# A new head for an attention and density kernel: 4 KB load rows, own tiles for the first keys, nine maxima moved into the stream, summed weights for the offsets

## The chip, the cores and the metric

The kernel runs on one core of a Trainium2 chip. The metric is device time in microseconds (us) of one execution. Engines are named as in the profile: PE (matrix products), PEld (its weight loads, which overlap PE), DVE (vector), ACT (scalar), POOL (GpSimd), SP (issues DMAs). ACT and POOL issue DMAs as well. Each engine runs its own instructions in program order and waits on semaphores for others.

## The reference

The input is `x`, 8 images of 192 channels and 64 x 64 = 4096 pixels, float32. Two layers, each added to its input; only the first is touched by the change.

```python
def _L0_conv_ref(x, w1, b1, a1, w2, b2, a2, wa, ba, aa):
    q = prelu(conv1x1(x, w1, b1), a1)      # 24 channels
    k = prelu(conv1x1(x, w2, b2), a2)      # 24 channels
    v = prelu(conv1x1(x, wa, ba), aa)      # 192 channels
    q = q.reshape(b, -1, hw).transpose(0, 2, 1)
    k = k.reshape(b, -1, hw)
    score = softmax(einsum('bnc,bcm->bnm', q, k), axis=2)
    v = v.reshape(b, c, hw).transpose(0, 2, 1)
    out = einsum('bnm,bmc->bnc', score, v)
    return out.transpose(0, 2, 1).reshape(b, c, h, w)

x = x + _L0_conv_ref(_gn(x), ...)
x = x + _L1_conv_ref(_gn(x), ...)
```

`_gn` normalises each of 32 groups of six channels by its mean and variance over all pixels. `_L1_conv_ref` pushes each value, once lowered and once raised by 0.5, through a chain of small per-channel layers with tanh and takes the absolute difference of two sigmoids.

## The kernel before

**Layout.** The 192 channels are held as 64 rows of three (`g`), and the pixels as two halves (`s`), so that 2 x 64 partitions are used. An image is cut into eight column parts `d` of 256 pixels per half; two parts make a chunk `c` of 512. A program planned step by step in Python (`at`, `job`, `work_off`) decides the order in which instructions stand on each engine; nothing is reordered on the chip.

**Head.** For the first image all is made at once. SP loads the eight parts (L97, two DMAs of 64 rows x 3 x 256 columns each) into buffers of the later density stage. `norm_stat` (L516) takes statistics, `norm_end` turns them into mean and scale `nrm` through two tiny products. `weights` (L603) scales the weights `wr` and `wa_sb` by `nrm` on ACT (L612), and computes the offsets that the mean gives to keys, queries (`bk`) and values (`ba`) by products over the three groups (L622, L627), with the already scaled weights. `keys` (L661) makes queries and keys of one part: products (L669), two Relus on ACT (L679), a DVE step (L684), and a split into a rounded part `kh` (L690, ACT) and its rest `kq` (L695, POOL); both go to DRAM (`kqd`, L687, on SP's queue). `fetch_keys` (L738) and `queries` (L722) read them back into four ring tiles `kr` and a tile `q`, in the layout of the score products. `values` (L771) makes a part's values: 24 products (L786), the offset added on DVE out of the product bank (L795), the slope on DVE (L800).

**Maxima.** Before a block of 512 queries can be scored, each query's largest score is needed. A block takes 16 maxima, each two products into a bank pair `mx` (L825) and one reduce on DVE (L833). `max_end` (L853) turns 16 of them into `rn`, stores it to DRAM (`nd`, L867) and reads it back as two rows of `q` (L871). The first maxima are made in the head, two at a time in the tiles `sc_head` and `mx_head`: `LEAD` = 25 of them.

**Stream.** 1024 steps `t`, 128 for an image, 16 for a block. In step `t` PE makes the scores of step `t + 1` (L896), one maximum of step `t + LEAD` (L825), and the attention of step `t` (L912, sixteen passes of 193 columns); ACT makes the exponentials (L901); DVE the reduce. Around them stand, by due times and credits, the loads, statistics, weights, keys and values of the next image, and on DVE, ACT and POOL the density layer of the image before. The credits take a job's PE time as room for DVE and ACT work (2.0 for the offset products). The `mx` tile exists once, and so does `sc`. The main loop is at L1634; small parameters of the density layer (`parameters`, L242) are computed in image 0 from step 4 on, from 22 table loads that SP issues in the head (L222).

**Completion of DMAs.** SP's and ACT's DMAs share eight completion semaphores; a DMA that gets one whose last user is under way is issued when that one has landed. An issue waits in its queue, and so does all behind it.

Of the kernel before, what the change touches and what calls it, by code (L numbers as in the profile page):

```python
# [18 lines left out]
def kernel(  # L19
# [30 lines left out]
    nc = tc.nc  # L50
# [70 lines left out]


    for d in range(NP):
        xi["first", 0, d] = bufs[3 + d][:, 0 : 3 * P].rearrange("p (g n) -> p g n", g=3)
        load(xi["first", 0, d], 0, d, P)

# [22 lines left out]
    wa_sb = const.tile([128, 3, C], F32, name="wa_sb")  # L149
    ba_all = const.tile([128, C], F32, name="ba_all")  # L150
    vslope = const.tile([128, 1], F32, name="vslope")
    nslope = const.tile([128, 1], F32, name="nslope")
# [7 lines left out]
    sa = st[:, 6 * CR : 6 * CR + 3 * C].rearrange("p (g o) -> p g o", g=3)  # L160
    sb = st[:, 6 * CR + 3 * C : 6 * CR + 4 * C]
    for s in range(2):
        p = slice(R * s, R * s + R)
        nc.scalar.dma_start(out=s1[p], in_=w1t.rearrange("(r g) o -> r g o", g=3))
        nc.scalar.dma_start(out=s2[p], in_=w2t.rearrange("(r g) o -> r g o", g=3))
        nc.scalar.dma_start(out=sa[p], in_=wat.rearrange("(r g) o -> r g o", g=3))
    nc.scalar.dma_start(out=sb, in_=ba.partition_broadcast(128))
    for k in range(4):
        b_ = b1 if k // 2 else b2
        nc.scalar.dma_start(out=bb[32 * k : 32 * k + CR], in_=b_.unsqueeze(1))  # L170
    for k in range(2):
        a = a1 if k else a2
        nc.scalar.dma_start(out=slope[64 * k : 64 * k + 64], in_=a.partition_broadcast(64))
    nc.scalar.dma_start(out=vslope, in_=aa.partition_broadcast(128))

# [12 lines left out]
    def spread():  # L188

        for k in range(4):  # L190
            p = slice(R * (k % 2), R * (k % 2) + R)
            nc.gpsimd.tensor_copy(wr[p, :, 32 * k : 32 * k + CR], (s1 if k // 2 else s2)[p])
        for g in range(3):
            nc.gpsimd.tensor_scalar(
                wa_sb[:, g, :].rearrange("p (h r) -> p h r", h=3),
                sa[:, g, :].rearrange("p (r h) -> p h r", h=3), vsign, None, ALU.mult,
            )
        nc.gpsimd.tensor_scalar(
            ba_all.rearrange("p (h r) -> p h r", h=3),
            sb.rearrange("p (r h) -> p h r", h=3), vsign, None, ALU.mult,  # L200
        )
# [12 lines left out]

    mm, cb, ff = table(24), table(10), table(9)
    for src, dst, at, n in (
        (m0, mm, 0, 3), (m1, mm, 3, 9), (m2, mm, 12, 9), (m3, mm, 21, 3),
# [385 lines left out]
    def weights(b, then):  # L603
# [3 lines left out]
        def scale():  # L607
            for k, src in (("k", wr), ("v", wa_sb)):
# [3 lines left out]
                nc.scalar.activation(d, src, AF.Copy, scale=res[:, 1:2])  # L612
            mb = cell["mb"] = fold.tile([128, 128], F32, tag="mb", name=f"mb_{b}")

            nc.vector.tensor_scalar(
                mb, res[:, 0:1].to_broadcast([128, 128]), 0.5, None, ALU.mult
            )

        def products():
            pf = cell["pf"]  # L620
            for g in range(3):
                cell["write"](nc.tensor.matmul(  # L622
                    pf[:, 0:2], lhsT=wf["k", b][:, g, :], rhs=res[:, 0:2],
                    start=g == 0, stop=g == 2,
                ))
            for g in range(3):
                cell["write"](nc.tensor.matmul(  # L627
                    pf[:, 4 : 4 + C], lhsT=cell["mb"], rhs=wf["v", b][:, g, :],
                    start=g == 0, stop=g == 2,
                ))  # L630

# [28 lines left out]

    def keys(b, d, what, done):  # L661

# [3 lines left out]
        def make(pk):  # L666
# [6 lines left out]
            done()  # L673
            kq = work.tile([128, P], F32, tag="kq", bufs=3, name=f"kq_{b}_{d}")
            kh = work.tile([128, P], F32, tag="kh", bufs=2, name=f"kh_{b}_{d}")

# [33 lines left out]

        job(make, d % 2)

# [57 lines left out]

    def values(b, d, what, done):  # L771

# [4 lines left out]
        def make(pv):  # L777
# [19 lines left out]
            def last():  # L797
# [3 lines left out]
                made.update(("v", b, d, k) for k in range(2))  # L801

            return [
                (0, lambda: None, 0.0, 0.0, 2.3), (1, first, 1.0, 0.0, 0.0),
                (2, last, 1.0, 0.0, 0.0),
            ]

        job(make, 0 if at_once else 1, 1 if what == "v" else 3, 2)

# [772 lines left out]

    for d in range(NP):
        for k in range(2):
# [12 lines left out]

    norm_end((0, 0), 2 * NP, 0, lambda: weights(0, lambda: None))
    settle()

    todo = [(keys, 2 * c + h) for c in ORDER for h in range(2)]
    todo += [(values, 2 * c + h) for c in ORDER for h in range(2)]
    ahead = deque([] for _ in range(13))
    ahead.extend(list(range(m, min(m + 2, LEAD))) for m in range(0, LEAD, 2))
    while todo or ahead:
        if todo:
            make, d = todo.pop(0)
            make(0, d, "first", lambda: None)
        if any(list(ahead)[:3]):
            del homes[2:]  # L1610
        pair = list(zip(others, ahead.popleft() if ahead else ()))
        for t, m in pair:
            max_products(*place(m), t)
        for t, m in pair:
            max_reduce(*place(m), t)
        if STEPS - 1 in [m for _, m in pair]:
            max_end(0, 0)
# [4 lines left out]
        if (0, 0) in kept and (0, 0) not in qt:  # L1622
            queries(0, 0)
        go_on()
    settle()
    assert not due and not loads
    now[0] = 0
    rest = parameters()
    stream[0] = True

    RATE = 4.15
    moves = plan_keys()
    scores(0)()
    for t in range(last):  # L1634
# [23 lines left out]
        attend(t)  # L1658
        work_off(t, RATE - 1.215)
    t = last  # L1660
# [42 lines left out]
```

## Time and profile before

| | |
|---|---|
| runs | 4350.76, 4351.48, 4351.46 us; median 4351.46 |
| profiled execution | 4350.1 us, span from the first to the last instruction 4348.1 |
| granted TensorE clock, mean | 0.986 of full speed |
| busy, share of the span | PE 97%, PEld 88%, DVE 89%, ACT 66%, POOL 26% |
| last load of the first image used by statistics | 20.67 us |
| first key product / first maximum / first score product | 30.0 / 63.4 / 104.5 us |

A view of stretches gives the busy time of each engine in it; the chain of work goes back from the last instruction, at each step to what released it; the timeline lists instructions in order of time, with the idle time before each and what ended it in brackets.

### The profile page before, as it was taken

The page shows a single profiled execution, that of the slowest core. Times are in us where ns is not written, and L with a number is a line of the kernel's source. Part 1 is how long each engine was busy: PE and PEld are TensorE (multiplying, and loading weights), DVE is VectorE, ACT ScalarE, POOL GpSimd, SP SyncE. Part 2 cuts the span into 40 slices and gives each one's busy share as a digit, 9 for nine tenths or more (in the row PEclk, how much of TensorE's full clock was granted, in tenths as well). Part 3 has the DMA queues.
Part 4 walks back from the last instruction along what each step waited for, and adds up shares of the span by engine and source line. Part 5 has one row for each costly group of instructions (what it writes and reads, how often), then busy time and mean ns, then how long its engine had stood idle before and what let it go on. Part 6 is the DMA issues. An engine that isn't in the chain of part 4 may idle for free.

```text
span 4348.1 us, 59628 instructions
## 1 busy us (share of the span) xinstructions
PE 4217.4 (97%) x23464; PEld 3810.4 (88%) x23464; DVE 3883.2 (89%) x4055; ACT 2848.1 (66%) x3104; POOL 1118.2 (26%) x1204
## 2 busy tenths in 40 slices
PE   7999999999999999999999999999999999999796
PEld 4999999999999999999999999999999998999432
DVE  5444359999999998999999999999999999999999
ACT  1333337776777767677677767777677767778775
POOL 1000001432223322342233322243133323333100
PEclk7999999999999999999999999999999999999898
DMA  3201133245343444336333442435333442324100
GB/s 80 43 26 42 37 73 71 67 83 98 76 83 75 93 97 83 64 65 118 80 87 67 86 108 62 88 76 105 83 82 71 87 92 52 70 48 73 25 15 15
DMA packets 239113, 309.55 MB, mean 71 GB/s; under 512 B 91249, under 2 KB 164849, under 8 KB 238833
## 3 DMA queue, kind: packets, MB, share of 16 engines
q1 hardware_dynamic: 201472, 173.15, 17.9%
q0 software_dynamic: 36288, 132.14, 17.3%
q8 instruction: 184, 3.01, 0.3%
q14 instruction: 97, 0.79, 0.1%
q10 hardware_dynamic: 1072, 0.47, 0.1%
HBM read 131.34 MB, written 42.21 MB: 40 GB/s over the span
## 4 chain that ended last, share of the span: by engine, by line
PE 55%; DVE 35%; ACT 4%; issue 3%; DMA 2%; POOL 1%; SPq 0%; DVEq 0%; POOLq 0%; ACTq 0%
PE b L912 37%; DVE d L1186 20%; DVE rm L833 9%; PE sc L896 7%; PE mx L825 7%; PE b L786 2%; DVE st L516 2%; PE b L669 1%; ACT e L901 1%; DMA xi<-in_x_dram 1%; DVE d L1144 1%; DVE xc L957 1%; DVE v L800 1%; DVE v L795 1%; DMA nd<-rn 0%
## 5 line engine op out<-in xcount | busy, mean ns | idle before, releaser
L912 PE MATMUL b<-v,e 128*128 128x193 f32 x16384 | 2844.8, 327 | 0.0
L912 PEld LDWEIGHTS b<-v,e 128*128 128x128 f32 x16384 | 2729.6, 190 | 90.7
L901 ACT ACTIVATE e<-sc 128x1024 f32<-128x1024 f32 x1024 | 1044.8, 1020 | 1198.4 <-PE sc L896 1194.2
L833 DVE TENSOR_REDUCE rm<-mx 128x1 f32<-128x1024 f32 x999 | 1216.2, 1217 | 369.9 <-PE mx L825 369.2
L1186 DVE SCALAR_TENSOR_TENSOR d<-d,un,d 128x1024 f32<-128x1024 f32 x1008 | 1302.2, 1312 | 14.7 <-ACT d L1180 8.8
L1186 DVE SCALAR_TENSOR_TENSOR d<-d,rt,d 128x1024 f32<-128x1024 f32 x684 | 875.7, 1293 | 6.6 <-PE b L1125 0.8
L896 PE MATMUL sc<-q,kr 98*128 98x512 f32 x2048 | 781.1, 462 | 12.3 <-ACT e L901 9.5
L1180 ACT ACTIVATE d<-d,bn,wn 128x1024 f32<-128x1024 f32 x504 | 617.7, 1235 | 69.5 <-DVE d L1186 68.8
L825 PE MATMUL mx<-kr,q 96*128 96x512 f32 x1998 | 637.3, 400 | 18.4 <-DVE rm L833 17.1
L1172 POOL DMA_DIRECT2D d<-xc x252 | 220.1, 906 | 1231.1 <-ACT d L1167 977.9
L825 PEld LDWEIGHTS mx<-kr,q 96*128 96x128 f32 x1998 | 370.2, 189 | 134.4 <-DVE rm L833 50.7
L1377 POOL MEMSET pause<- 128x1 f32 x456 | 61.6, 135 | 1313.6 <-DVE d L1186 1313.5
L896 PEld LDWEIGHTS sc<-q,kr 98*128 98x128 f32 x2048 | 355.1, 191 | 39.0 <-ACT e L901 20.2
L1158 ACT ACTIVATE d<-xc,bn,wn 128x1024 f32<-128x1024 f32 x288 | 349.9, 1232 | 7.6 <-DVE bn L582 7.6
L1228 POOL TENSOR_TENSOR d<-d,d 128x512 f32<-128x512 f32 x168 | 325.7, 1940 | 39.5 <-ACT d L1222 38.2
L1167 ACT ACTIVATE d<-d,un 128x1024 f32<-128x1024 f32 x252 | 282.2, 1141 | 0.0
L695 POOL TENSOR_TENSOR kq<-kq,kh 128x256 f32<-128x256 f32 x64 | 85.3, 1333 | 380.3 <-ACT kh L690 379.7
L1429 POOL TENSOR_TENSOR d<-d,d 128x512 f32<-128x512 f32 x80 | 161.0, 2012 | 0.0
L1437 POOL TENSOR_TENSOR d<-d,d 128x512 f32<-128x512 f32 x80 | 158.2, 1977 | 1.6
L1416 POOL TENSOR_TENSOR d<-d,d 128x512 f32<-128x512 f32 x80 | 152.2, 1903 | 0.0
L1421 ACT ACTIVATE d<-d,bn,wn 128x512 f32<-128x512 f32 x160 | 121.4, 808 | 39.9 <-POOL d L1416 32.1
L786 PE MATMUL b<-wv,xi 64*128 64x192 f32 x1344 | 124.4, 331 | 0.6 <-DVE v L795 0.4
(196 smaller groups left out, 2156.8 us busy)
## 6 DMA issues: line engine op xcount, KB each, us to landing
d<-xc POOLq DMA_DIRECT2D x252, 512.0 KB, 5.4
xi<-in_x_dram SPq DMA_DIRECT2D x280, 192.0 KB
kr<-kqd SPq DMA_DIRECT2D x352, 96.0 KB
xc<-in_x_dram SPq DMA_DIRECT2D x64, 384.0 KB
out_dram<-xc SPq DMA_DIRECT2D x94, 256.0 KB
q<-kqd SPq DMA_DIRECT2D x128, 96.0 KB
kqd<-kh SPq DMA_DIRECT2D x64, 128.0 KB
kqd<-kq SPq DMA_DIRECT2D x64, 128.0 KB
```

The lines of the kernel that those rows point to most:

```text
L786: nc.tensor.matmul(pv[:, s, k, :], lhsT=t[p, g, k * 128 : k * 128 + 128], rhs=wf["v", b][p, g, :], start=g == 0 and k == 0, stop=g == 2, s ...
L825: nc.tensor.matmul(sc[:, s, :], lhsT=tile_of(qt[b, n // 2], n, j)[0 : 4 * CR].bitcast(F32R), rhs=keys_of(b, c)[0 : 4 * CR, s, :].bitcast(F ...
L833: nc.vector.tensor_reduce(out=rowmax[b, n][:, j, k : k + 1], in_=sc, axis=AX.XY, op=ALU.max)
L896: nc.tensor.matmul(sc[:, s, :], lhsT=keys_of(b, ORDER[p // 4])[r, s, k : k + 128].bitcast(F32R), rhs=qt[b, n // 2][r, :, u : u + 256].bitc ...
L901: return lambda: nc.scalar.activation(e, sc, AF.Exp)
L912: nc.tensor.matmul(a[:, j, 0 : C + 1], lhsT=e[:, s, j * 128 : j * 128 + 128], rhs=v[:, s, p % 4, :], start=p == 0 and s == 0 and j % 2 == ...
L1158: nc.scalar.activation(self.buf[k], self.src(), AF.Tanh, bias=bn[:, s, g, i : i + 1], scale=wn[:, g, i : i + 1],)
L1167: nc.scalar.activation(dst, self.buf["t", 0, 0], AF.Copy, scale=norms[b, 1][1][:, g, 3 * i : 3 * i + 1])
L1172: nc.gpsimd.dma_start(out=dst, in_=x_, accum_op=ALU.add)
L1180: nc.scalar.activation(self.buf[k], self.buf["l", n, k[2]], AF.Tanh, bias=norms[b, 1][2][:, s, g, i : i + 1], scale=self.scales()[0][:, g, ...
L1186: recent.append(nc.vector.scalar_tensor_tensor(dst, src, factor, dst if plus is None else plus, ALU.mult, ALU.add))
L1228: return nc.gpsimd.tensor_tensor(z[:, n], z[:, n], dst[:, n], ALU.add)
```

## The change

- The first image is loaded by twelve DMAs of 64 rows x 1024 columns, one group at a time, into six buffers; the class `Early` gives the parts `d` as slices of them. Statistics are taken over 512 columns, twelve times.
- On ACT's queue the loads of the slopes stand first. `signs` and `spread` stand ahead of the statistics.
- `wr_sum` and `wa_sum` hold the weights summed over the three groups (POOL). The offsets become one product each: `wr_sum` with mean times scale (`mr`), `wa_sum` with half of it (`mb`).
- In the head each key part has tiles of its own (in `bufs[11..14]`), and `kh` goes to DRAM on ACT's queue. Which part takes which bank and when is written out in a table (`start`), the maxima in another (`found`).
- In the head, values are copied out of the bank by ACT and the offset is added by POOL; DVE makes the slope (`last`) for four parts after the last reduce of the head, for two in the stream. The last two parts are made in the stream as ordinary jobs.
- The head makes 16 maxima in place of 25. In the stream, each step makes one, and from step 2 on a second after the attention until 25 steps of lead are reached (steps 2 to 10).
- The 22 table loads are issued one per step from step 10 on; `parameters` starts after step 40.

```diff
+    class Early:
+        def __init__(self, d):
+            self.q, self.at = d // 4, d % 4 * P
+
+        def __getitem__(self, key):
+            p, g, n = key
+            return bufs[3 + 3 * self.q + g][
+                p, self.at + (n.start or 0) : self.at + (n.stop or P)
+            ]
+
+    for q in range(2):
+        for g in range(3):
+            for s in range(2):
+                k = s * N // 2 + q * 2 * F
+                nc.sync.dma_start(
+                    out=bufs[3 + 3 * q + g][R * s : R * s + R], in_=xv[0, :, g, k : k + 2 * F]
+                )
     for d in range(NP):
-        xi["first", 0, d] = bufs[3 + d][:, 0 : 3 * P].rearrange("p (g n) -> p g n", g=3)
-        load(xi["first", 0, d], 0, d, P)
+        xi["first", 0, d] = Early(d)
...
+        for dst, src in ((wr_sum, wr), (wa_sum, wa_sb)):
+            nc.gpsimd.tensor_tensor(dst, src[:, 0, :], src[:, 1, :], ALU.add)
+            nc.gpsimd.tensor_tensor(dst, dst, src[:, 2, :], ALU.add)
...
-            nc.sync.dma_start(
-                out=dst[R * s : R * s + R, :, at : at + n],
-                in_=src.rearrange("(r g) i j -> r g (i j)", g=3),
-            )
+            tables.append((
+                dst[R * s : R * s + R, :, at : at + n],
+                src.rearrange("(r g) i j -> r g (i j)", g=3),
+            ))
...
-            mb = cell["mb"] = fold.tile([128, 128], F32, tag="mb", name=f"mb_{b}")
+            mr = cell["mr"] = fold.tile([128, 2], F32, tag="mr", name=f"mr_{b}")
             nc.vector.tensor_scalar(
-                mb, res[:, 0:1].to_broadcast([128, 128]), 0.5, None, ALU.mult
+                mr, res[:, 0:1].to_broadcast([128, 2]), res[:, 1:2], None, ALU.mult
+            )
+            mb = work.tile([128, P], F32, tag="kh", bufs=2, name=f"mb_{b}")[:, 0:128]
+            cell["mb"] = mb
+
+            nc.vector.tensor_scalar(
+                mb, mr[:, 0:1].to_broadcast([128, 128]), 0.5, None, ALU.mult
             )
 
         def products():
             pf = cell["pf"]
-            for g in range(3):
-                cell["write"](nc.tensor.matmul(
-                    pf[:, 0:2], lhsT=wf["k", b][:, g, :], rhs=res[:, 0:2],
-                    start=g == 0, stop=g == 2,
-                ))
-            for g in range(3):
-                cell["write"](nc.tensor.matmul(
-                    pf[:, 4 : 4 + C], lhsT=cell["mb"], rhs=wf["v", b][:, g, :],
-                    start=g == 0, stop=g == 2,
-                ))
+
+            cell["write"](nc.tensor.matmul(
+                pf[:, 0:2], lhsT=wr_sum, rhs=cell["mr"], start=True, stop=True
+            ))
+            cell["write"](nc.tensor.matmul(
+                pf[:, 4 : 4 + C], lhsT=cell["mb"], rhs=wa_sum, start=True, stop=True
+            ))
...
-            return [(0, products, 0.0, 0.0, 2.0), (1, offsets, 1.0, 0.0, 0.0)]
+            return [(0, products, 0.0, 0.0, 0.6), (1, offsets, 1.0, 0.0, 0.0)]
...
+            if begin:
+                kq, kh = (bufs[11 + d // 2][:, (2 * (d % 2) + i) * P :][:, 0:P] for i in range(2))
+            else:
+                kq = work.tile([128, P], F32, tag="kq", bufs=3, name=f"kq_{b}_{d}")
+                kh = work.tile([128, P], F32, tag="kh", bufs=2, name=f"kh_{b}_{d}")
...
-                nc.sync.dma_start(out=kqd[b % 2][i, c, :, h * P : h * P + P], in_=src)
+                queue = nc.scalar if begin and i == 0 else nc.sync
+                queue.dma_start(out=kqd[b % 2][i, c, :, h * P : h * P + P], in_=src)
...
+            def copy():
+                nc.scalar.activation(v[:, :, :, 0:C], pv, AF.Copy)
+                pieces.append(with_offset)
+
+            def with_offset():
+                offset = wf["ba", b].unsqueeze(1).unsqueeze(1).to_broadcast([128, 2, 2, C])
+                nc.gpsimd.tensor_tensor(v[:, :, :, 0:C], v[:, :, :, 0:C], offset, ALU.add)
+                raw.append(last)
...
-    for d in range(NP):
-        for k in range(2):
-            norm_stat((0, 0), 2 * d + k, flat(xi["first", 0, d], k))
     signs()
     spread()
+    for n in range(12):
+        norm_stat((0, 0), n, bufs[3 + n // 2][:, n % 2 * F : n % 2 * F + F])
...
+    T0, T1, SC, MX = range(4)
+    start = {
+        0: (keys, 0, T0, 0), 1: (keys, 1, T1, 0), 2: (keys, 4, SC, 0), 3: (keys, 5, MX, 0),
+        4: (values, 0, T0, None), 5: (keys, 2, T1, 0), 6: (keys, 3, SC, 0),
+        7: (values, 1, T0, None), 8: (keys, 6, T1, 0), 9: (keys, 7, T1, 1),
+        11: (values, 4, T0, None), 13: (values, 5, T1, None),
+        17: (values, 2, T0, None), 18: (values, 3, T1, None),
+    }
+    found = {8: 0, 9: 2, 10: 4, 11: 6, 12: 8, 13: 10, 15: 12, 16: 14}
+    left = [4]
+    k = 0
+    while k < 20 or pieces:
+        if k in found:
+            pair = list(zip(others, (found[k], found[k] + 1)))
+            for t, m in pair:
+                max_products(*place(m), t)
+            for t, m in pair:
+                max_reduce(*place(m), t)
+            if k == 16:
+                max_end(0, 0)
+        if k in start:
+            make, d, n, i = start[k]
...
+            make(0, d, "first", lambda: None, begin)
+        go_on()
+        if k > 16:
+            while raw and left[0]:
+                raw.popleft()()
+                left[0] -= 1
         for i, c in enumerate(ORDER):
             if (0, c) not in kept and all(("kq", 0, 2 * c + h) in made for h in range(2)):
+                if i == 0:
+                    queries(0, 0)
                 fetch_keys(0, c, i)
-                break
...
+    for d in (6, 7):
+        values(0, d, "first", lambda: None)
+    found = STEPS
...
-        if 3 < t < IMG:
+        if 10 <= t < 10 + len(tables):
+            dst, src = tables[t - 10]
+            nc.sync.dma_start(out=dst, in_=src)
+        if 40 < t < IMG:
             next(rest, None)
+        if raw and t > 2:
+            raw.popleft()()
...
-        max_step(t + LEAD)
+        max_step(found)
+        found += 1
         if run:
             run()
         attend(t)
+        if t > 1 and found <= t + LEAD:
+            max_step(found)
+            found += 1
```

More of the change, by code (lines that the diff above doesn't have):

```diff
@@ L150 @@
     ba_all = const.tile([128, C], F32, name="ba_all")
+    wr_sum = const.tile([128, 128], F32, name="wr_sum")
+    wa_sum = const.tile([128, C], F32, name="wa_sum")
     vslope = const.tile([128, 1], F32, name="vslope")
@@ L161 @@
     sb = st[:, 6 * CR + 3 * C : 6 * CR + 4 * C]
+    nc.scalar.dma_start(out=vslope, in_=aa.partition_broadcast(128))
+    for k in range(2):
+        a = a1 if k else a2
+        nc.scalar.dma_start(out=slope[64 * k : 64 * k + 64], in_=a.partition_broadcast(64))
     for s in range(2):
@@ L170 @@
         nc.scalar.dma_start(out=bb[32 * k : 32 * k + CR], in_=b_.unsqueeze(1))
-    for k in range(2):
-        a = a1 if k else a2
-        nc.scalar.dma_start(out=slope[64 * k : 64 * k + 64], in_=a.partition_broadcast(64))
-    nc.scalar.dma_start(out=vslope, in_=aa.partition_broadcast(128))
     vtiles = []
@@ L215 @@
     mm, cb, ff = table(24), table(10), table(9)
+    tables = []
     for src, dst, at, n in (
@@ L659, with keys @@
         kqd.append(t)
-    def keys(b, d, what, done):
+    def keys(b, d, what, done, begin=None):
         t = xi[what, b, d]
@@ L673, in make @@
             done()
-            kq = work.tile([128, P], F32, tag="kq", bufs=3, name=f"kq_{b}_{d}")
-            kh = work.tile([128, P], F32, tag="kh", bufs=2, name=f"kh_{b}_{d}")
+            if begin:
[3 more added lines that the diff above has]
+                kh = work.tile([128, P], F32, tag="kh", bufs=2, name=f"kh_{b}_{d}")
             def first():
@@ L709, in make @@
             ]
-        job(make, d % 2)
+        if begin:
+            begin(make)
+        else:
+            job(make, d % 2)
     def part_of(b, c, i, k):
@@ L769, in plan_keys, with values @@
         return moves
-    def values(b, d, what, done):
+    raw = deque()
+    def values(b, d, what, done, begin=None):
         t = xi[what, b, d]
@@ L801, in last @@
                 made.update(("v", b, d, k) for k in range(2))
+            def copy():
[5 more added lines that the diff above has]
+                raw.append(last)
+            if begin:
+                return [(1, copy, 0.0, 0.0, 0.0)]
             return [
@@ L806, in make @@
             ]
-        job(make, 0 if at_once else 1, 1 if what == "v" else 3, 2)
+        if begin:
+            begin(make)
+        else:
+            job(make, 0 if at_once else 1, 1 if what == "v" else 3, 2)
     rowmax = {}
@@ L1580, in within @@
             at(t + 64 * c + 6, lambda fetch=fetch: request("xc", fetch))
-    for d in range(NP):
-        for k in range(2):
-            norm_stat((0, 0), 2 * d + k, flat(xi["first", 0, d], k))
     signs()
     spread()
+    for n in range(12):
+        norm_stat((0, 0), n, bufs[3 + n // 2][:, n % 2 * F : n % 2 * F + F])
     homes.extend((t, [0, 0]) for t in turns + others)
@@ L1596, in settle @@
             go_on()
-    norm_end((0, 0), 2 * NP, 0, lambda: weights(0, lambda: None))
+    norm_end((0, 0), 12, 0, lambda: weights(0, lambda: None))
     settle()
[L1601 to L1617, printed above, removed]
+    T0, T1, SC, MX = range(4)
@@ new lines, with begin @@
+    start = {
[19 more added lines that the diff above has]
+            make, d, n, i = start[k]
+            def begin(parts, n=n, i=i):
+                spot[0] = n, i or 0
+                pm = (turns + others)[n]
+                for o, fn, *cost in parts(pm if i is None else pm[:, i, :]):
+                    at(now[0] + o, fn, *cost)
+            make(0, d, "first", lambda: None, begin)
[4 more added lines that the diff above has]
+                left[0] -= 1
@@ L1618 @@
         for i, c in enumerate(ORDER):
             if (0, c) not in kept and all(("kq", 0, 2 * c + h) in made for h in range(2)):
+                if i == 0:
+                    queries(0, 0)
                 fetch_keys(0, c, i)
-                break
-        if (0, 0) in kept and (0, 0) not in qt:
-            queries(0, 0)
-        go_on()
+        k += 1
     settle()
@@ L1629 @@
     stream[0] = True
+    assert not pieces and len(raw) == 2
+    for d in (6, 7):
+        values(0, d, "first", lambda: None)
+    found = STEPS
     RATE = 4.15
```

## The prediction

> **What bounds the kernel now.** I read the engines' busy time in stretches first, then the chain of work that ended last, then the timeline of the head and of the first stream steps. The columns of the first view are: stretch, its length, busy time of PE, PEld, DVE, ACT, POOL, granted clock, DMA share, GB/s.
>
> ```profile
> 0.00:20.00 20.00, 15.55 (x32) 6.64 (x32) 8.50 (x24) 1.28 (x1) 5.40 (x14) 1.00 0.74 181
> 40.00:60.00 20.00, 12.63 (x96) 11.04 (x96) 4.15 (x7) 7.42 (x17) 4.32 (x6) 0.83 0.41 126
> 60.00:80.00 20.00, 15.40 (x127) 11.68 (x124) 19.93 (x21) 0.00 (x0) 0.00 (x0) 0.99 0.18 60
> 80.00:100.00 20.00, 16.19 (x29) 6.74 (x29) 19.00 (x21) 0.00 (x0) 0.00 (x0) 0.50 0.02 0
> 200.00:300.00 100.00, 100.00 (x587) 94.04 (x587) 41.89 (x75) 34.53 (x46) 2.18 (x3) 1.00 0.10 28
> ```
>
> There are two regimes. Up to 104.5 us, the head, the bound changes hands: the load (0 to 20), round trips of the keys through DRAM (30 to 58, no engine full), DVE (60 to 92), one DMA trip. After it PE is full and, in the first image, DVE is 42% busy. The chain shows the joints (start, length, what):
>
> ```profile
> 26.95 1.44 PE b L622 x6
> 28.39 2.13 PE b L627 x6
> 30.52 1.99 PE sc_head L669 x6
> ...
> 89.47 2.37 DVE rm L833 x2
> 92.46 9.70 DMA nd<-rn
> 102.17 2.19 DMA q<-nd
> 104.49 1.21 PE sc L896 x2
> ...
> 217.52 0.56 PE b L622 x6
> 218.08 1.08 PE b L627 x6
> ```
>
> The trip `rm` to DRAM and back into `q` lasts from 92.46 to 104.49, 12.03 us. Maxima 16 to 24, the nine that are moved, run inside it (92.35 to 103.71): they end nothing. What they will cost in the stream is read from the one place where a stream step waits for a reduce:
>
> ```profile
> 151.44 1.22 DVE L833 TENSOR_REDUCE rm<-mx 128x1 f32<-128x1024 f32 x1
> ...
> 152.71 0.73 PE L825 MATMUL mx<-kr,q 96*128 96x512 f32 x2 [0.89 <-DVE rm L833]
> ```
>
> **The head, part by part.** I call N the moment when the first image's mean and scale are ready (26.2 before: last statistics end 21.7, then the chain of small DVE and PE steps) and T0 the first score product (104.5).
>
> *Load.* Twelve transfers of 256 KB replace sixteen of 192 KB; issue is 0.6 us each. In the changed program each from the third on first waits for an earlier transfer that used the same completion semaphore, four times a small one of ACT's queue (`w2t`, issued 1.30, was used at 5.18: 3.9 us; the SP queue's waits show such holds before too, 2.3 us on `wat`). Followed through, the last issue comes at about 12. The bytes (3.15 MB plus 0.46 MB of weights) at the best 1.5 us slice of the trace's DMA view, 273 GB/s, need 13.2 us after some 2 us until the first have landed (the 4 KB of q<-nd take 2.19): not before 15. I take 16.5 for the last landing; the other end is the old 20.7. Statistics of 512 columns are not in the trace; 384 take 0.51, so 0.68, two after the last landing. N = 16.5 + 1.4 + 4.2 (the aggregate at 21.91 to 26.19) = 22.1, bounds 20.6 and 26.3. The weight work on POOL (four more adds) starts when `wa` lands, near 12, and needs 2.5 + 0.8 + about 2 (a 128x256 add takes 0.73) + 0.8: over by 18, hidden unless N falls below that.
>
> *Offsets.* L622 and L627 shrink from six matmuls (two passes each over three groups) to two: 3.57 to 1.19 us on the cold array, and they no longer wait for ACT's 0.6 us scaling. DVE gains one operation of 0.16.
>
> *Keys.* Before, ACT waits five times, 14.7 us together, for `kqd` writes that hold a tile. Own tiles remove that. From N: offsets until 1.45; first two keys 2.2 each (cold, as L669 at 30.0), then 1.46. ACT's pair of Relu takes 0.84, DVE's step 0.49, the copy 0.41, an issue 0.4. ACT's queue now also issues the `kh` writes, behind the next pair of Relu: the second one goes out at N + 10.2, lands 2.0 later (1.8 to 3.1 in the trace), then SP issues four `q` and four `kr` loads (1.61 + 2.01) and the last lands about 2.1 after issue. First maxima at N + 18 = 40.1 (63.4 before); bounds 16 and 21.
>
> *Sixteen maxima.* The 2.28 us for two reduces, 0.75 until the first, two key steps of DVE between: d7's own step ends 11.3 later. Then copy 0.41, a value copy on ACT (128x768; between L936's 0.42 for 192 columns and L901's 1.02 for 1024: 0.85), issue 0.4, landing 2.0, four `kr` issues 2.0, landing 2.1: ring 3 is there at 19.2, and DVE has been idle for some 3 us. Product and four reduces 5.4, `rn` 0.5: the store is issued 25.1 after the first maximum, against 20.5 if ring 3 were in time. The value copies and POOL's six adds (128x768, 2.2 to 2.9 us each by L695 and L1228) lie beside this. The trip stays 12.03: it now covers four `v` steps on DVE (4.1 us), where before it covered nine maxima. T0 = 40.1 + 25.1 + 12.0 = 77.2. **Head: 27.3 us less**; 20 to 33 by the bounds.
>
> [...] The row comes first: at 80 to 100 the array, with no gap above 1 us, was already granted 0.50, and 0.61 from 104.5 to 112, so the first two steps are cold in both kernels, difference 0. [...]
>
> **The stream.** A step is 3.56 us of PE: scores 0.47, maximum 0.47, attention 2.62. In steps 2 to 10 a second maximum follows the attention: 9 x 0.47 = 4.2. There is one `mx` tile, so the next step's first maximum stands behind the reduce of that one: it can start 0.04 + 1.22 + 0.05 = 1.31 after its end, the scores cover 0.47, and the refill costs 0.26 (0.73 against 0.47): 1.1 a step. It is paid in steps 3 and 6 to 11, 7.7; after steps 3 and 4 the products of the two remaining value tiles stand between and hide it. These cost 2 x 2.15 = 4.3, and the second pair waits 2.8 for DVE (reduce 1.26, a statistic 0.55, the `v` add 0.95 that frees its bank). In step 6 DVE's queue (two statistics, `v` step, `v` add) delays a reduce, 1.1 more. Sum 20.1. Bounds: 8.5 if only products count, 26 if each of ten waits also holds a statistic. Behind the waiting PE stand attention and ACT's Exp; nobody else waits long.
>
> Two SP steps move here: 22 table loads, one issue of 0.6 per step of 4 us, and they stand in the queue between the second block's `nd` store and its return. Before, that trip took 29.8 from `rn` to use and needed 19.5 (3 of queue, 13.8, 2.2 and 0.5); now 24 to 27 are left. It is covered; each us beyond would be a us of PE. The wait at 150.8 on `xi` (3.9 of DVE, 1.2 of PE) goes, since longer steps give the loads time. **Stream: 20.1 - 1.2 = 18.9 more.**
>
> **The other seven images.** Offsets fall from 1.64 to 0.55 of PE, 1.1 each. The first two lie where PE is the bound: 2.2. Later DVE is busy 499 of 510 us, so little comes through; and with less PE time in the plan the DVE operations of later images stand in slightly different order, which I can only bound: nothing up to 7.6 gained, or 4 lost. I take 3 gained.
>
> Sum: -27.3 + 18.9 - 3 = -11.4. Against the profiled execution, 4350.1 (span 4348.1 and 2.0 around it), 4338.7; the median of the runs is 1.4 above it: **4340**.
>
> **Rivals.** First, *the stream takes the nine maxima almost for nothing*: waits overlap, and products alone count (8.5 instead of 20.1). For it: DVE is 42% busy there. Against it: one `mx` tile, and 0.89 of idle PE in the row above. 4340 - 11.6 = 4328. Second, *the keys' round trips still set the head*: load at 20.7, each landing 3.1 instead of 2.0 on a longer SP queue, head only 20 us less; 4347, no change that can be told. For it: ACT's queue carries issues before Relus. Third, slower: *the clock falls in steps 2 to 11*, since PE now idles once per step. Step work 4.02 becomes 8.04, with the value products ten steps take about 92 instead of 56: 4376. It decides from three to four steps at half clock on (4 us each against a gain of 11). Against it: from 60 to 80, PE had such gaps every 4 us and was granted 0.99.
>
> **How the numbers follow.** Forecast 0.52, first rival 0.22, second 0.18, third 0.08. A measurement here tells 0.2% (8.7 us) from no change. The forecast's own range, 4332 to 4348, lies some three quarters below 4342.8: faster 0.39 + 0.22 = 0.61, same 0.13 + 0.18 = 0.31, slower 0.08. The range takes in both near rivals: 4326 to 4352.
>
> **What would show it.** Right: statistics ending near 18, first maxima near 40, a DVE gap before the last four head maxima, the `nd` trip from 65 to 77, steps of 5.1 us with PE waits on `rm` of about 0.85 in the first ten, clock 1.00 there. Wrong: loads landing after 20, steps of 4.0, PE waiting for `q<-nd` at the second block, or clock rows of 0.5 after 80.

## The result, and the profile after

The changed kernel takes 4362.14 us, median of 15 runs (4356.35 to 4366.44); on the same chip the kernel before takes 4351.77 (4349.24 to 4355.36, 15 runs). The ratio is 1.0022, interval 1.0015 to 1.0029: 0.22% or 10.4 us slower, where 11.4 us faster had been forecast. The profiled execution of the changed kernel took 4356.35 us (span 4354.6), the lowest of its runs, 6 us under their median.

First the stretches of the changed kernel that answer to those shown of before (columns as there):

```profile
0.00:20.00 20.00, 16.57 (x32) 6.94 (x32) 8.71 (x23) 1.28 (x1) 11.58 (x28) 1.00 0.74 181
40.00:60.00 20.00, 15.16 (x78) 10.56 (x78) 14.07 (x15) 4.77 (x11) 6.27 (x7) 0.91 0.45 142
60.00:80.00 20.00, 8.72 (x80) 6.84 (x78) 13.00 (x13) 3.72 (x4) 6.28 (x3) 0.87 0.06 13
80.00:100.00 20.00, 17.26 (x75) 15.20 (x76) 6.58 (x6) 5.12 (x5) 0.00 (x0) 0.79 0.32 80
200.00:300.00 100.00, 100.00 (x586) 94.02 (x585) 41.99 (x61) 34.38 (x48) 2.19 (x3) 1.00 0.12 33
```

The load moves the same 181 GB/s in the first 20 us as before. The wait for the maxima's trip has moved from 92-104 into the stretch 60:80, where TensorE is now half empty. From 200 on, in the first image, nothing has changed: PE is full.

The joints of the head in the chain of waits of the changed kernel (start, length, what):

```profile
15.24 4.90 DMA d<-in_x_dram
20.24 1.30 DVE st L539 x2
...
26.09 0.56 PE b L650 x2
26.65 0.85 PE b L653 x2
...
43.85 0.97 PE sc_head L873 x2
...
62.78 4.63 DVE rm L881 x4
...
68.03 10.63 DMA nd<-rn
78.67 1.97 DMA q<-nd
80.78 1.21 PE sc L944 x2
```

Statistics still wait for the load at 20.24. The offsets (L650, L653) are short; the maxima start at 43.85 and the first score product comes at 80.78, where before it came at 104.49: the head is 23.7 us shorter. And the stream, in the timeline of PE:

```profile
134.56 0.76 PE L873 MATMUL mx<-kr,q 96*128 96x512 f32 x2
135.16 0.64 PE L944 MATMUL sc<-q,kr 98*128 98x512 f32 x2
136.63 0.73 PE L873 MATMUL mx<-kr,q 96*128 96x512 f32 x2 [0.84 <-DVE rm L881]
137.21 2.78 PE L960 MATMUL b<-v,e 128*128 128x193 f32 x16
```

A step has two products `mx`, and the first of them waits 0.84 us for the reduce of the one before, as was forecast: steps are 5.13 us long.

So head and stream did roughly what they should. To see where the rest went I read, in both traces, the reciprocal that ends each of the 64 attention blocks (L932 before, L980 after). In the table the changed kernel's time is given as its difference to before, us; images 2 to 8 begin with blocks 8, 16, ... 56:

| end of block | 0 | 1 | 7 | 11 | 15 | 22 | 31 | 39 | 47 | 55 | 63 | span |
|---|---|---|---|---|---|---|---|---|---|---|---|---|
| after - before | -2.3 | -3.4 | -3.3 | -2.2 | +1.0 | +3.4 | +2.6 | +6.9 | +6.9 | +9.1 | +7.5 | +6.5 |

The first image ends 3.3 us early and keeps this to block 7. The seven later images lose 10.8; the prediction had given them, together with block 1's offsets, a gain of 3. There the density work of ScalarE, VectorE and GpSimd runs beside attention. The waits in the stretch 600 to 4060, in which all of this lies (waiting, for whom: us in total, times, longest), first of before, then of the changed kernel:

```profile
DVE rm L833 <- PE mx L825: 89.6, 107, 3.0
```

```profile
DVE rm L881 <- PE mx L873: 95.4, 99, 4.1
...
PE mx L873 <- DMA kr<-kqd: 5.4, 2, 4.0
```

VectorE, busy 3337 of these 3460 us in both kernels, waits 5.8 us more for the array's maxima, and the array waits 5.4 us for keys, a wait that before does not have.

### The profile page after: what moved, and what is told of

The parts are those of the page before. It is cut to its first block, busy times and chain, and to the rows that moved or that the text cites. A ratio compares the mean times of both kernels' runs of the same rounds, so it can differ in the third digit from the quotient of the medians.

```text
span 4354.6 us, 59465 instructions
## 1 busy us (share of the span) xinstructions
PE 4207.6 (97%) x23400; PEld 3799.0 (87%) x23400; DVE 3884.9 (89%) x4053; ACT 2853.6 (66%) x3110; POOL 1134.9 (26%) x1214
## 4 chain that ended last, share of the span: by engine, by line
PE 53%; DVE 39%; ACT 3%; issue 2%; DMA 2%; POOL 0%; SPq 0%; ACTq 0%; DVEq 0%; POOLq 0%
PE b L960 36%; DVE d L1234 22%; DVE rm L881 10%; PE mx L873 7%; PE sc L944 7%; PE b L820 2%; DVE st L539 2%; PE b L694 1%; DVE d L1192 1%; DVE xc L1005 1%; DVE v L834 1%; ACT e L949 1%; DVE v L829 1%; DVE xc L1527 1%; PE b L994 0%
## 5 line engine op out<-in xcount | busy, mean ns | idle before, releaser
L944 PE MATMUL sc<-q,kr 98*128 98x512 f32 x2048 | 780.1, 462 | 22.8 <-ACT e L949 11.6
L873 PE MATMUL mx<-kr,q 96*128 96x512 f32 x2016 | 646.5, 402 | 32.0 <-DVE rm L881 23.0
L1220 POOL DMA_DIRECT2D d<-xc x252 | 221.9, 916 | 1270.1 <-ACT d L1215 991.1
L1276 POOL TENSOR_TENSOR d<-d,d 128x512 f32<-128x512 f32 x168 | 324.3, 1931 | 34.9 <-ACT d L1270 31.0
L1485 POOL TENSOR_TENSOR d<-d,d 128x512 f32<-128x512 f32 x80 | 165.7, 2072 | 1.8 <-ACT e L949 0.3
L724 POOL TENSOR_TENSOR kq<-kq,kh 128x256 f32<-128x256 f32 x56 | 75.1, 1341 | 335.8 <-ACT kh L719 334.7
L1464 POOL TENSOR_TENSOR d<-d,d 128x512 f32<-128x512 f32 x80 | 158.8, 1994 | 0.5 <-issue 0.5
L1477 POOL TENSOR_TENSOR d<-d,d 128x512 f32<-128x512 f32 x80 | 157.8, 1973 | 0.2 <-issue 0.2
L820 PE MATMUL b<-wv,xi 64*128 64x192 f32 x1344 | 124.4, 331 | 1.8 <-DVE v L829 1.8
```

Source lines behind the costliest of these rows:

```text
L820: nc.tensor.matmul(pv[:, s, k, :], lhsT=t[p, g, k * 128 : k * 128 + 128], rhs=wf["v", b][p, g, :], start=g == 0 and k == 0, stop=g == 2, s ...
L873: nc.tensor.matmul(sc[:, s, :], lhsT=tile_of(qt[b, n // 2], n, j)[0 : 4 * CR].bitcast(F32R), rhs=keys_of(b, c)[0 : 4 * CR, s, :].bitcast(F ...
L944: nc.tensor.matmul(sc[:, s, :], lhsT=keys_of(b, ORDER[p // 4])[r, s, k : k + 128].bitcast(F32R), rhs=qt[b, n // 2][r, :, u : u + 256].bitc ...
L1220: nc.gpsimd.dma_start(out=dst, in_=x_, accum_op=ALU.add)
L1276: return nc.gpsimd.tensor_tensor(z[:, n], z[:, n], dst[:, n], ALU.add)
```

## The experiments

Ratios are to the kernel before on the same chip; before took 4361.4 us beside the first four kernels, 4350.8 beside the second four, 4361.6 beside the two quarter kernels and the last two of this section, and 4351.4 beside the sliver kernels and `before06_again`, so times are compared within one group.

**Which part loses the later images.** The diff touches them in one place: the offsets of every image. They got two matmuls in place of six, and with that a smaller number in the plan, the time of PE that the step gives to the balance of ScalarE and VectorE (2.0 to 0.6). In the changed kernel and in before with that one number changed, ScalarE's, VectorE's and GpSimd's instructions stand in the same order from the second image on (but for one small VectorE operation of the offsets), and in another than in before; with 2.0 the order is that of before, whatever the head. Four kernels take number and products apart:

```diff
 # after_credit2 (the changed kernel)
-            return [(0, products, 0.0, 0.0, 0.6), (1, offsets, 1.0, 0.0, 0.0)]
+            return [(0, products, 0.0, 0.0, 2.0), (1, offsets, 1.0, 0.0, 0.0)]
 # before_credit06 (the kernel before)
-            return [(0, products, 0.0, 0.0, 2.0), (1, offsets, 1.0, 0.0, 0.0)]
+            return [(0, products, 0.0, 0.0, 0.6), (1, offsets, 1.0, 0.0, 0.0)]
 # before_sums: before, with wr_sum, wa_sum and the two short products, number 2.0
 # before_sums06: the same, number 0.6
```

> The changed kernel with one number put back: the offset products count 2.0 of PE time in the plan, as before, in place of 0.6. From the second image on its DVE, ACT and POOL instructions then stand in the order of the kernel before. Theory (the order): the new head is 3.3 us ahead at the end of the first image (block 7: 599.1 against 602.3 in the profiles), and the reordered density work of the later images loses some 10 to 14. Then this run is ahead of the kernel before by 3 to 9 us: 4343 to 4349 at a median of 4352 for before. Rival (the short offsets themselves, their extra DVE step or the tile shared with the keys): the loss stays, 4357 to 4366. Rival (the head: stream shifted, parameters later): it stays too.

Measured: 4360.07 us, ratio 0.9994 (0.9985 to 1.0002).

> The kernel before with one number changed: the offset products count 0.6 in the plan in place of 2.0; nothing else. Theory (the order): the loss of the later images shows alone, 8 to 14 us, 4360 to 4366. Both rivals: 4350 to 4354, as before.

Measured: 4380.56 us, ratio 1.0042 (1.0029 to 1.0055).

> The kernel before with the summed weights and the two-product offsets, at the old count of 2.0; the order of all later work is that of before. Theory (the order): a gain of 1 to 8 us, 1.1 of PE in each of seven images and 1 in the head, as far as PE is the bound: 4344 to 4351. Rival (the short offsets themselves cost): 4357 or more. Rival (the head): as the theory.

Measured: 4360.81 us, ratio 0.9996 (0.9987 to 1.0005).

> Summed weights and the count of 0.6 in the kernel before: the whole of the change that reaches the later images, with the old head. Theory (the order): 4 to 13 us slower, 4356 to 4365. Rival (the short offsets): the same. Rival (the head): 4344 to 4352, no loss without the new head.

Measured: 4377.45 us, ratio 1.0031 (1.002 to 1.0042).

The number alone, with not one instruction added or taken away, makes the kernel before 19 us slower (4380.6 against 4361.4); beside the short products it costs 16.6 (4377.5 against 4360.8). Both are more than the 8 to 14 and 4 to 13 that I had expected. The short products themselves bring 0.6, which can't be told from nothing. This settles which part loses. The changed kernel with the old number is level with before and not 3 to 9 us faster as I had expected: what its head and stream leave (3.3 us in the trace) is near the limit of the measurement.

**Is the head's gain kept, where nothing is paid for it?** Three kernels carry the old number and make all 25 maxima in the head, the nine further ones inside the trip of the first maxima through DRAM; two of them also make all eight value parts there. The changed kernel ran beside them.

```diff
 # max_head (the changed kernel, number 2.0)
-    found = {8: 0, 9: 2, 10: 4, 11: 6, 12: 8, 13: 10, 15: 12, 16: 14}
+    found = {8: 0, 9: 2, 10: 4, 11: 6, 12: 8, 13: 10, 15: 12, 16: 14,
+             17: 16, 18: 18, 19: 20, 20: 22, 21: 24}
...
-    found = STEPS
+    found = LEAD
 # full_head, in addition
+        20: (values, 6, T0, None), 21: (values, 7, T1, None),
...
-    left = [4]
+    left = [2]
...
-    for d in (6, 7):
-        values(0, d, "first", lambda: None)
 # full_two_queues, in addition
-                nc.sync.dma_start(
+                (nc.scalar if s else nc.sync).dma_start(
```

> The changed kernel once more, on the chip of the three runs beside it. The order theory (the smaller offset credit gives the other seven images a worse order of DVE and ScalarE work): 4 to 15 us above before (ratio 1.001 to 1.0035), and above the same kernel with the old credit; the granted clock near 0.99, maxima that VectorE waits for some 5 us more than before over the stream. If the loss of the other images belonged to the new head or stream and not to that number, the new head with the old credit and everything in it would lose as much after the first image as this one does.

Measured: 4363.64 us, ratio 1.0024 (1.0015 to 1.0033).

> Old credit of 2.0; all 25 maxima and all eight value products stand in the head, the nine further maxima after the store of the first block's maxima, six of eight value slopes in the stream. Order theory with the steps priced as the changed kernel showed them (steps of 5.1 while a second maximum is made, two values 2.15 each): TensorE has 9 x 0.86 + 2 products of values of some 1.3 in the 12.7 us after the store, so scores can start at 82 (81 to 84), the stream runs at the pace of before, the lead over before is 21 at block 0 and about as much at block 7, and the order of all later images is that of before: 14 to 24 us faster than before, ratio 0.9945 to 0.997. Rival, a sink: the later images give back what the first one saves, since the changed head with the old credit kept only 1.3 us of its 5 at block 7: 1 to 6 us faster, ratio 0.9985 to 1.000.

Measured: 4332.65 us, ratio 0.9957 (0.9945 to 0.997).

> Old credit of 2.0; as the last one, but only the nine maxima stand in the head, and values 6 and 7 are jobs of the stream as in the changed kernel. Order theory: the second maxima cost the stream 9 x 0.47 and the waits of 0.85 to 1.1 that steps 3 to 11 showed (12 to 16 us), the two values 4.3 and their waits: 12 to 19 us faster than before, 2 to 6 above the kernel with all values in the head. Rival, a sink: 0 to 5 us faster, and the two kernels alike within 2.

Measured: 4337.83 us, ratio 0.9968 (0.9955 to 0.998).

> As the kernel with everything in the head, but the twelve loads of the first image are issued six by SyncE and six by ScalarE, ahead of the weights, instead of twelve by SyncE, which took 15.1 us to issue. If the issue sets the last landing (20.2 of which 15.84 is the last issue), it comes near 13 and the norm near 19, 5 to 7 us less: 18 to 30 us faster than before. Rival: the transfers set it (1.5 MB in 20 us), or the weights that now come 6 us later do: landing within 2 us of 20, and no gain over the kernel with one queue. With a sink behind both: within 2 us of each other at the end, however early the norm.

Measured: 4338.77 us, ratio 0.9967 (0.9955 to 0.998).

The ends of the blocks, as differences to the first table's trace of before (before's median on the two chips is 4350.8 and 4351.8):

| end of block | 0 | 7 | 15 | 23 | 31 | 47 | 63 |
|---|---|---|---|---|---|---|---|
| after_again (0.6) | +1.0 | 0.0 | +4.7 | +10.7 | +9.6 | +15.3 | +15.9 |
| full_head (2.0) | -18.8 | -19.8 | -20.3 | -20.0 | -20.5 | -20.2 | -20.0 |
| max_head (2.0) | -11.1 | -12.0 | -11.9 | -11.2 | -11.7 | -11.6 | -10.8 |

With the old number a lead of 20 or 12 us goes through seven images unchanged, within 1.3 us (`full_two_queues`, with the old number too, gives back up to 2.1 of its 12): there is no sink in which a shorter head is lost. With 0.6 the kernel loses 16 us after block 7, in the same images as in its first trace. `full_head` is the version that beats both: 18 us (0.4%) under before. Its first score product comes at 85.23, 4.4 us later than in the changed kernel's first trace, and at block 7 it is 16.5 ahead of it: the nine maxima and two value parts had cost the stream 21 us. Beside `after_again`, on the same chip, the sum is the same: 1.2 later at the first score product (84.05 there), 19.8 ahead at block 7. Its chain of waits shows what they cost in the head:

```profile
64.05 4.63 DVE rm L881 x4
68.72 1.03 PE mx_head L873 x2
69.75 3.46 PE b L820 x24
...
83.15 2.17 PE b L820 x24
```

From 69 to 85 TensorE makes maxima and value parts (L820) one after the other; a trip of 12.75 from the store at 69.30 would have been over at 82. So the added work costs the head 3.2 us there. The two-queue kernel failed at a place of its own: the slopes' loads stood behind six image loads on ScalarE's queue, and VectorE's first small operation on them held all statistics. From its timeline of VectorE:

```profile
15.25 0.15 DVE L203 TENSOR_SCALAR vsign<-vslope 128x1 f32<-128x1 f32 x1 [11.92 <-DMA vslope<-in_aa_dram]
...
15.79 7.22 DVE L539 BATCH_NORM_STATS2 st<-d 128x6 f32<-128x512 f32 x12
```

So twelve statistics ran back to back until 23.0, later than the 21.9 to 22.5 of the others beside it. Before the last four maxima VectorE waited 3.9 us, while TensorE made a value part ahead of them in 4.1 us (granted clock 0.62 from 60 to 69, where `full_head` had 1.00), and the head was 7.5 us longer than that of `full_head`.

**How the order costs.** One place in the trace shows a candidate. GpSimd's accumulating loads `d<-xc` (DMAs that add what they carry to the tile `d`; 512 KB each, L1172 before, L1220 after) each follow a copy by ScalarE. The timelines of GpSimd, and for the changed kernel also SyncE's issues and one product, about 1490 to 1512, the same step of the same block (the store of the maxima, 1493.7) in both kernels; first before, then the changed kernel:

```profile
1492.47 0.86 POOL L1172 DMA_DIRECT2D d<-xc  x1 [28.61 <-ACT d L1167]
...
1497.94 0.87 POOL L1172 DMA_DIRECT2D d<-xc  x1 [0.21 <-POOL d L1228]
...
1506.71 0.87 POOL L1172 DMA_DIRECT2D d<-xc  x1
```

```profile
1492.62 0.87 POOL L1220 DMA_DIRECT2D d<-xc  x1
...
1493.71 0.39 SPq L915 DMA_DIRECT2D nd<-rn  x1
1493.90 0.85 POOL L1220 DMA_DIRECT2D d<-xc  x1 [0.41 <-issue]
1494.20 5.27 SPq L770 DMA_DIRECT2D kr<-kqd  x4
...
1496.29 0.86 POOL L1220 DMA_DIRECT2D d<-xc  x1
...
1511.55 0.93 PE L873 MATMUL mx<-kr,q 96*128 96x512 f32 x2 [4.03 <-DMA kr<-kqd]
```

The changed kernel issues three such loads within 3.7 us, beside the store and the fetch of keys; before, they are spread over 14. By the view of DMA issues in 1490 to 1512 (count, size, median us from issue to landing), before and then after:

```profile
d<-xc POOLq DMA_DIRECT2D x3, 512.0 KB, 6.4
```

```profile
d<-xc POOLq DMA_DIRECT2D x3, 512.0 KB, 13.5
```

The loads take twice as long, and the next maximum product waits 4.03 us for keys. The plan fetches keys four steps, 14 us, ahead of use. To test it, the accumulating loads were cut, in both orders, to a quarter of their columns and to a sliver of 32; the instructions and their order stay.

```diff
-                nc.gpsimd.dma_start(out=dst, in_=x_, accum_op=ALU.add)
+                w = F // 2        # quarter; F // 16 for the sliver
+                nc.gpsimd.dma_start(out=dst[:, 0:w], in_=x_[:, 0:w], accum_op=ALU.add)
```

> The kernel before, with each accumulating load of d<-xc on GpSimd's queue cut to a quarter of its columns (512 KB of traffic to 128; three quarters of the sum are left out). The order of instructions is that of before. If those loads cost the stream anything in the old order, it is little, since no fetch of keys waits behind them there: 0 to 8 us below before.

Measured: 4358.53 us, ratio 0.9993 (0.9985 to 1.0002).

> The same cut (three quarters of the sum left out) in the kernel before with the offset credit of 0.6, whose full version stood 18 us above before. Collision theory (the new order lets accumulating loads come in bunches together with the fetches of keys and maxima, which then land late and hold TensorE): with a quarter of the traffic the distance to the other quarter kernel falls to 0 to 6 us. Rival (the new order of DVE and ScalarE instructions costs by itself, by reduces that come late between other VectorE work): the distance stays at 12 to 20 us.

Measured: 4365.64 us, ratio 1.0011 (1.0002 to 1.002).

> The kernel before with each accumulating load of d<-xc cut to 32 of 1024 columns (16 KB instead of 512; the rest of the sum is left out). As the quarter kernel stood 3 us below before, this one should stand 2 to 6 below.

Measured: 4352.01 us, ratio 1.0000 (0.9991 to 1.0009).

> The same cut (the rest of the sum is left out) with the offset credit of 0.6. With a quarter of the traffic 7 us of 18 were left between the orders. If what was left is traffic too, the distance to the other sliver kernel is now 0 to 4 us; if it belongs to the order of the instructions on the engines, it stays at 5 to 9.

Measured: 4356.38 us, ratio 1.0011 (1.0002 to 1.002).

> The kernel before with the offset credit of 0.6 and its loads whole, on the chip of the sliver kernels: 12 to 20 us above before, ratio 1.003 to 1.0045, as on the other chip; this is the distance that the two slivers are held against.

Measured: 4366.30 us, ratio 1.0034 (1.0021 to 1.0048).

> The changed kernel as it is (0.6), with the same cut of the accumulating loads (the rest of the sum is left out). Its head and stream stand some 1 to 3 us under before at block 7. If traffic is what its later images lose by, it stands 0 to 5 us under the sliver of before; if the order by itself, 2 to 8 above it.

Measured: 4353.44 us, ratio 1.0005 (0.9996 to 1.0014).

| distance between the orders, kernel with 0.6 less kernel with 2.0 | us |
|---|---|
| whole loads, first and last group | 19.2 and 14.9 |
| quarter | 7.1 |
| sliver (last group) | 4.4 |

In the old order the loads' traffic costs nothing (the quarter is 3.1 us under before, the sliver 0.6 above, both within the measurement). In the new order it costs 10.5 of 14.9 us, and its removal takes the changed kernel from 10 to 13 us above before to 2. So the loads' traffic is some two thirds of it, shown; the array's waits for keys in the stretch 600 to 4060 go the same way, from 7.4 us in `before06_again` to 0.9 in `before06_sliver`. Neither theory met its ranges: the quarter's 7.1 and the sliver's 4.4 fall between the two, the changed kernel's sliver (1.4 above that of before) does too, and the sliver of before is not 2 to 6 below before. 4.4 us remain with next to no traffic (runs of 4355.5 to 4358.9 against 4350.1 to 4353.9), so a part belongs to the order on the engines or to other transfers.

The ends of the blocks in the kept traces (one execution each, that of before from the first chip) say where the two parts lie. What the new order loses in them, us:

| kernel less kernel | blocks 8 to 15 | block 22 | all others from 16 to 63 |
|---|---|---|---|
| before06_again less before | 6.0 | 6.3 | 5.2 |
| before06_sliver less before_sliver | 5.8 | -1.2 | 2.5 |
| after less before | 4.2 | 4.6 | 1.9 |
| after_sliver less before_sliver | 4.3 | -1.2 | -0.7 |

The traffic acts almost in one place, block 22, which is the step shown above: between `before06_again` and `before06_sliver`, two runs on one chip, 7.5 us lie in it. The array waits 4.4 us there for keys, and more follows from the clock, as PE's timeline and the stretch after the wait show in `before06_again`:

```profile
1517.35 1.19 PE L825 MATMUL mx<-kr,q 96*128 96x512 f32 x2 [4.44 <-DMA kr<-kqd]
1518.34 5.26 PE L912 MATMUL b<-v,e 128*128 128x193 f32 x16
```

```profile
1517.30:1525.00 7.70, 7.65 (x26) 7.32 (x27) 4.05 (x4) 0.84 (x1) 2.18 (x2) 0.60 0.55 146
```

The granted clock was 1.00 from 1505 to 1512 and 0.60 from 1517.3 to 1525; the attention after the wait took 5.26 us in place of 2.78, the product 1.19 in place of 0.63. Wait and slow step are together 7.5 us. The image from block 8 to 15 loses the same with the traffic and without it, 6 us (4 in the changed kernel). From 602 to 1098 the array's waits rise there by 3.7 us from `before_sliver` to `before06_sliver`: for reduces from 0.6 to 2.6, for exponentials from 1.2 to 2.0, for keys from 0 to 0.9. Which instructions hold these reduces, and where the rest lies, stays open.

**The old number once more, and the loads on two engines.** In `full_head_loads` SyncE issues nine loads of the first image and ScalarE the last three, behind the weights.

```diff
 # full_head_loads (full_head)
+                part = bufs[3 + 3 * q + g][R * s : R * s + R], xv[0, :, g, k : k + 2 * F]
+                if q * s:
+                    late.append(part)
+                else:
+                    nc.sync.dma_start(out=part[0], in_=part[1])
...
+    for out, in_ in late:
+        nc.scalar.dma_start(out=out, in_=in_)
```

> The changed kernel with the old credit of 2.0 again, so that its later images have the order of before. The kernels with everything in the head kept their lead over before to the end, flat within 1.5 us from block 7 on; by the order theory this one too keeps what it has at block 7 (about 1 to 5 us under before), while the changed kernel with 0.6 lost 11 to 16 from there on: 1 to 6 us faster than before, ratio 0.9985 to 0.9998. Rival, a loss that belongs to second maxima in the stream and not to the number: slower than before after block 7, ratio 1.001 or more.

Measured: 4358.49 us, ratio 0.9995 (0.9986 to 1.0003).

> Everything in the head, old credit, and the first image's loads issued by two engines: nine by SyncE, the last three by ScalarE behind the weights of the first image. The two-queue kernel showed the loads done by 15 us at 230 to 257 GB/s, and its statistics held back by a wait for the slopes. Here nothing stands ahead of the statistics: last landing 15 to 17 instead of 20, the norm at 21 to 23 instead of 26, T0 near 79, 2 to 5 us under the kernel with twelve loads on SyncE, 18 to 27 under before. Rival: the key fetches and the maxima that follow are not held by the norm, and T0 stays within 1 us.

Measured: 4345.68 us, ratio 0.9963 (0.9949 to 0.9976).

The changed kernel with 2.0 is again level with before, 3.1 us under it. Issuing the last three loads by ScalarE behind the weights brought nothing: the kernel is 15.9 us under before, where 18 to 27 had been expected, and the norm (mean and scale) is ready at 26.7 as in `full_head` (26.2). SyncE's own timeline shows that its queue became no shorter:

```profile
0.72 16.70 SPq L143 DMA_DIRECT2D d<-in_x_dram  x9
```

Nine issues took longer than twelve did (15.11 in the changed kernel), and from 2 to 14 us the rate is the same, 204 GB/s against 202 in `full_head`. The waits of SyncE's queue say what holds the issues, DMAs that still have the completion semaphore: 8.5 us in the changed kernel, of which 6.9 for loads of weights, offsets and slopes on ScalarE's queue, and 11.7 us here. That a second issuer frees nothing does not follow. In `full_two_queues`, where six image loads stand first on either queue, SyncE's six were issued in 7.4 us, and 263 GB/s were moved from 2 to 14 us, 3.16 MB and so as much as the whole image (3.15 MB, not the 1.5 of its expectation); from 14 to 15 us the rate was 31. What an earlier landing is worth is not shown, since the statistics stood behind the slopes there; the slopes first and then six image loads on each queue were not run.

## Why the prediction was wrong, step by step

Its sum was -11.4; the profiled executions differ by +6.5 in span. Of the 17.9 us between them, 11.8 are one term.

| step | forecast | in the trace | off by |
|---|---|---|---|
| norm ready, N | 22.1 | 25.7 | 3.6 |
| first maxima after N | 18 | 18.2 | 0.2 |
| store after the first maximum | 25.1 | 24.2 | -0.9 |
| the trip | 12.0 | 12.8 | 0.7 |
| head | -27.3 | -23.7 | 3.6 |
| stream | +18.9 | +21.4 | 2.5 |
| other images | -3 | +8.8 | 11.8 |

- **The step that failed** is "The other seven images": "the DVE operations of later images stand in slightly different order, which I can only bound: nothing up to 7.6 gained, or 4 lost. I take 3 gained." The first half was right: block 1 shows the forecast 1.1 us of a shorter offset. But the order is not slightly different, and its price was put at 4 us at most, with nothing in the trace of before to set that bound. Alone it costs 15 to 19 us, in the changed kernel 11 to 16 after block 7. It was looked for on VectorE alone. Some two thirds of it is the traffic of GpSimd's accumulating loads, which go in a bunch in the new order and meet a fetch of keys in block 22; the other part is there without the traffic, and some of it is waits of the array for VectorE's reduces.
- **The load** was mis-sized. I took its rate from the best slice, 273 GB/s; the rows from 0 to 20 said 181 for the whole stretch, and they say so after. Longer rows changed nothing: the last landing is 20.1 where I had 16.5. The holds of SyncE's queue, which I had followed through, were put too low: the last issue began at 15.2, not at about 12, while the rate itself was nearly reached (263) where each of two queues had six loads. My bound for N (26.3, the old landing) held.
- **Keys, offsets, maxima and trip** were right within 1 us each: the gap of VectorE before the last four maxima is there (1.46 us, where I had some 3), the maxima begin 18.2 after N, and the emptied trip is not shorter. That the nine maxima had run free inside that trip was also right, and `full_head` and `max_head` show it from the other side: put back there, they give the stream's cost back.
- **The stream** was right in its mechanism and nearly in size: steps of 5.13 with waits of 0.84, clock 1.00 from 120 on. The first two steps are 0.9 us longer than before's, which I had at no difference: from 80.8 to 89.5 the granted clock was 0.56, where before had 0.61 from 104.5 to 112. That the emptied trip cost these 0.9 us is not shown: the array was busy 2.2 of 13 us in it, but in `max_head` 12.6 of 16, and there the first two steps took 8.40 us, as the changed kernel's did (8.39; before 7.47). The row of before from 80 to 100 was also misread: the array stood still for 1.72 us up to 82.5, so there was a gap above 1 us where the clock was 0.50.
- **The rivals.** The second (keys' round trips set the head, 20 us less) was near for the head, and half by its cause: the load landed near the old time, as it said, but the first maxima came 18.2 after N, as the forecast had it. The slower one, a falling clock in the stream, came only for a moment: the granted clock was 1.00 from 89.5 to 110, 0.83 from 110 to 120 and 1.00 from 120 to 136, where three to four steps at half clock would have decided it. The case that came, a new order in later images that costs more than the head brings, was not among them.

## What to carry to other kernels

A cost that a planner is told is part of the program: correcting one number can reorder every later stage, so list the new order against the old and treat the change as two, the edit and the number; here the edit was worth nothing measurable and the number lost 15 to 19 us. Where an order changes, look at what it does to the spacing of transfers before pricing engine time; one meeting of three loads and a fetch cost 7.5 us. And a round trip that the end of a stage waits for is the place to put work: nine maxima and two value parts cost 21 us in a stream where TensorE is full (100 of 100 us from 200 to 300), and 3.2 beyond the 12.8 us of the trip.

## What the runs showed of the hardware that was not expected

- Three accumulating loads of 512 KB within 3.7 us took a median of 13.5 us to land in place of 6.4. In that time the DMA engines were busy and moved little; the changed kernel's stretches are below (the last three columns are granted clock, DMA share and GB/s). That little is moved is not the bunch's doing alone: before shows 54 and 34 GB/s in the same stretches, at shares of 0.92 and 0.61.

```profile
1498.00:1502.00 4.00, 4.00 (x24) 3.82 (x24) 4.00 (x7) 2.72 (x4) 1.33 (x2) 1.00 1.23 83
1502.00:1506.00 4.00, 4.00 (x25) 3.82 (x24) 4.00 (x5) 3.70 (x5) 2.17 (x2) 1.00 1.10 57
```

- The first image's load runs at the same rate with the longer rows as with those of before: 204 and 202 GB/s from 2 to 14 us. With half of it issued by each of two engines, ahead of the weights, it reached 263 in that time.
- A wait of TensorE cost more than its length: in block 22 of `before06_again`, after 4.44 us without work, the granted clock was 0.60 for the next 7.7 us, and 7.5 us were lost in all.
